# Row norm of an attention layer as a lagged stream of half blocks, and its scores, bias and extreme in one VectorE operation

## The chip, the cores and the metric

The kernel runs on one core of one Trainium2 chip. The metric is device time in microseconds, from start to end of one launch. Before the change it is 35310.41 us (median of three runs, 35305.11 to 35334.66). All data is fp32. The engines are TensorE (matmul, PE in the profile; its weight loads are PEld), VectorE (DVE), ScalarE (ACT), GpSimd (POOL) and SyncE (SP), which issues the DMAs.

## What is computed

Four residual layers over an image of 256 x 256 positions with 128 channels. Each layer normalises its input by groups of 4 channels over all positions, and adds its result to the input. The change is in the first layer, an attention along rows with a norm over channels in front of it:

```
x = x + layer0(group_norm(x))          # then layers 1, 2, 3 in the same way

def layer0(z_ij, ln_gamma, ln_beta, Wq, Wk, Wv, Wb, Wg, Wout):
    mu  = mean(z_ij, channels);  var = variance(z_ij, channels)
    z   = (z_ij - mu) * rsqrt(var + 1e-5) * ln_gamma + ln_beta
    q, k, v = heads(z @ Wq), heads(z @ Wk), heads(z @ Wv)     # 4 heads of 32
    bias = z @ Wb                                             # 4 numbers a position
    g = sigmoid(heads(z @ Wg))
    scores = einsum('bijhd,bikhd->bijkh', q, k) / sqrt(32) + bias[:, None]
    a = softmax(scores, over k)
    o = g * einsum('bijkh,bikhd->bijhd', a, v)
    return o @ Wout
```

The other layers are a selective scan in four directions, a spectral mixing and a recurrence. Most of the time is the scan's; it isn't touched.

## The kernel before

Channels lie on the 128 partitions and positions along the free dimension. An early pass (`stream_stats`, L76) reads all of x and collects statistics; `group_norm_coef` (L52) makes of them one scale and one shift per channel, `ab`. Then `layer0` (L89) has two stages.

**Row norm** (L106 to L142). A loop over 32 blocks of 2048 positions. Per block: load x (L113); VectorE applies the group norm's scale and shift (L114); then for each of four chunks of 512, TensorE multiplies by `cent`, the identity minus 1/128, which takes off the mean over channels (L120, into PSUM); VectorE copies that to `d` in SBUF (L121), ScalarE squares the same PSUM tile (L123), and TensorE averages the squares over channels into one of four groups of 32 partitions of `var` (L124). ScalarE takes the root (L128), VectorE the reciprocal (L129). Then again for each chunk TensorE spreads the reciprocal over the partitions (L135, a matmul with one row of ones), VectorE multiplies (L136), GpSimd applies gamma and beta (L137), TensorE makes the 4 bias rows (L139) and ScalarE copies them (L140). Two DMAs store z and bias to DRAM (L141, L142). Here the scheduler of the language orders the instructions of each engine; the order on each engine is that of the timelines, with two blocks interlaced.

**Attention** (`attention`, L147). It works in 512 units: 32 blocks of 8 image rows, of each row two pairs of heads. The order is written out by hand (`manual_schedule`): at step u every engine's queue gets, one after the other,
- `scores(u + 2)` (L207 to L222): TensorE's four score matmuls into a PSUM tile of 4 x 256 elements, in which the head changes with every matmul; VectorE adds the bias (L215) and takes the negated maximum of each row of 256 (L222);
- `exps(u + 1)`: ScalarE's four exponentials with that maximum as bias, each with its sum over the row (L228); VectorE's reciprocal of the four sums (L231); GpSimd multiplies by it (L232);
- `transposes(u)`: TensorE's eight transposes (L240); ScalarE copies one half (L243), VectorE the other (L245);
- one or, in units 5 to 9 of a block, two `project` calls for the next block (L188, L193; in units 5 to 15);
- `product(u - 1)`: TensorE's four matmuls with v (L254), two heads, each over two halves of k that add up in PSUM; the two heads write different groups of 32 partitions;
- every second unit `gate` (L268), every fourth `out` (L281 to L283), the output matmul, the residual and its statistics.

A matmul of fp32 is two records of the trace. The constants that occur below: `c.ones`, `c.avg128` (all 1/128), `w` (the five weights), `NPOS` = 65536, `CH` = 512.

Of the kernel before, what the change touches and what calls it, by code (L numbers as in the profile page):

```python
# [10 lines left out]
F32 = mybir.dt.float32  # L11
AF = mybir.ActivationFunctionType
ALU = mybir.AluOpType
AX = mybir.AxisListType
PSUM = bass.MemoryType.PSUM
DRAM = bass.MemoryType.DRAM

P = 128
S = 256
NPOS = S * S  # L20
CH = 512
# [24 lines left out]
def load(nc, pool, src, name):  # L46
    to = pool.tile(list(src.shape), F32, name=name)
    nc.sync.dma_start(to, src)
    return to
# [38 lines left out]

def layer0(c, x, x1, ab, stats):  # L89
    tc, nc, t = c.tc, c.nc, c.t  # L90
    BL = 2048
    NB = NPOS // BL
    NH = 4
    with ExitStack() as ctx:
        dram = ctx.enter_context(tc.tile_pool(name="l0_dram", bufs=1, space=DRAM))
        wp = ctx.enter_context(tc.tile_pool(name="l0_w", bufs=1))
        zs = dram.tile([P, NPOS], F32, name="l0_z")
        bs = dram.tile([NH, S, S], F32, name="l0_bias")
        cent = load(nc, wp, t["c_cent"], "l0_cent")
        wb = load(nc, wp, t["l0_wb"], "l0_wb")  # L100
        gamma = load(nc, wp, t["l0_gamma"], "l0_gamma")
        beta = load(nc, wp, t["l0_beta"], "l0_beta")
        w = {n: load(nc, wp, t[f"l0_w{n}"], f"l0_w{n}") for n in "qkvgo"}


        with ExitStack() as a:  # L106
            io = a.enter_context(tc.tile_pool(name="l0a_io", bufs=3))
            wk = a.enter_context(tc.tile_pool(name="l0a_wk", bufs=2))
            ps = a.enter_context(tc.tile_pool(name="l0a_ps", bufs=2, space=PSUM))
            for b in range(NB):  # L110
                sl = bass.ts(b, BL)
                xt = io.tile([P, BL], F32, name="l0a_x")
                nc.sync.dma_start(xt, x[:, sl])  # L113
                nc.vector.tensor_scalar(xt, xt, ab[:, 0:1], ab[:, 1:2], ALU.mult, ALU.add)  # L114
                d = wk.tile([P, BL], F32, name="l0a_d")
                var = ps.tile([P, CH], F32, name="l0a_var")
                for j in range(4):
                    cs = bass.ts(j, CH)
                    dp = ps.tile([P, CH], F32, name="l0a_dp")
                    nc.tensor.matmul(dp, cent, xt[:, cs], start=True, stop=True)  # L120
                    nc.vector.tensor_copy(d[:, cs], dp)  # L121
                    sq = wk.tile([P, CH], F32, name="l0a_sq")
                    nc.scalar.activation(sq, dp, AF.Square)  # L123
                    nc.tensor.matmul(  # L124
                        var[32 * j : 32 * j + 32], c.avg128[:, 0:32], sq, start=True, stop=True
                    )
                rs = wk.tile([P, CH], F32, name="l0a_rs")
                nc.scalar.activation(rs, var, AF.Sqrt, bias=c.eps)  # L128
                nc.vector.reciprocal(rs, rs)  # L129
                bias = wk.tile([NH, BL], F32, name="l0a_bias")  # L130
                for j in range(4):
                    cs = bass.ts(j, CH)
                    r = slice(32 * j, 32 * j + 1)
                    bc = ps.tile([P, CH], F32, name="l0a_bc")
                    nc.tensor.matmul(bc, c.ones[r], rs[r], start=True, stop=True)  # L135
                    nc.vector.tensor_tensor(d[:, cs], d[:, cs], bc, ALU.mult)  # L136
                    nc.gpsimd.tensor_scalar(d[:, cs], d[:, cs], gamma, beta, ALU.mult, ALU.add)  # L137
                    bp = ps.tile([NH, CH], F32, name="l0a_bp")
                    nc.tensor.matmul(bp, wb, d[:, cs], start=True, stop=True)  # L139
                    nc.scalar.copy(bias[:, cs], bp)  # L140
                nc.sync.dma_start(zs[:, sl], d)  # L141
                nc.sync.dma_start(bs.rearrange("h j k -> h (j k)")[:, sl], bias)  # L142

        attention(c, x, x1, zs, bs, w, stats)


def attention(c, x, x1, zs, bs, w, stats):  # L147
# [3 lines left out]
    tc, nc = c.tc, c.nc  # L151
    BL, NH = 2048, 4
    NB = NPOS // BL
    UB = 16
    N = UB * NB
    with ExitStack() as a:
        one = a.enter_context(tc.tile_pool(name="l0b_one", bufs=1))
        io = a.enter_context(tc.tile_pool(name="l0b_io", bufs=2))
        wk = a.enter_context(tc.tile_pool(name="l0b_wk", bufs=2))
        ps2 = a.enter_context(tc.tile_pool(name="l0b_p2", bufs=2, space=PSUM))  # L160
        ps1 = a.enter_context(tc.tile_pool(name="l0b_p1", bufs=1, space=PSUM))
        bias = one.tile([P, NH, 2, S], F32, name="l0b_bias")
# [9 lines left out]
        def load_block(b):  # L172
            k = blocks[b] = {}
            for n, src in (("z", zs), ("x", x)):
                k[n] = io.tile([P, BL], F32, name=f"l0b_{n}")
                nc.sync.dma_start(k[n], src[:, bass.ts(b, BL)])
            for n in "qkg":
                k[n] = wk.tile([P, BL], F32, name=f"l0b_{n}")
            k["v"] = wk.tile([P, 16, P], F32, name="l0b_v")
# [21 lines left out]
        def scores(u):  # L201
            k, r, hp = blocks[u // UB], u % UB // 2, u % 2
            sc = ps2.tile([P, 2, 2, S], F32, name="l0b_sc")
            for jt in range(2):
                for h in range(2):
                    hs = slice(32 * (2 * hp + h), 32 * (2 * hp + h) + 32)
                    nc.tensor.matmul(  # L207
                        sc[:, h, jt],
                        k["q"][hs, bass.ds(r * S + jt * P, P)],
                        k["k"][hs, bass.ts(r, S)],  # L210
                        start=True,
                        stop=True,
                    )
            e = es[u] = wk.tile([P, 4, S], F32, name="l0b_e", bufs=4)
            nc.vector.tensor_tensor(  # L215
                e,
                sc.rearrange("p h j k -> p (h j) k"),
                bias[:, 2 * hp : 2 * hp + 2].rearrange("p h j k -> p (h j) k"),
                ALU.add,
            )  # L220
            top = tops[u] = wk.tile([P, 4], F32, name="l0b_top")
            nc.vector.tensor_reduce(top, e, AX.X, ALU.max, negate=True)  # L222

        def exps(u):
            e, top = es[u], tops.pop(u)
            den = wk.tile([P, 4], F32, name="l0b_den")
            for i in range(4):
                nc.scalar.activation(  # L228
                    e[:, i], e[:, i], AF.Exp, bias=top[:, i : i + 1], accum_out=den[:, i : i + 1]
                )  # L230
            nc.vector.reciprocal(den, den)  # L231
            nc.gpsimd.tensor_tensor(e, e, den[:, :, None].to_broadcast([P, 4, S]), ALU.mult)  # L232
# [14 lines left out]
        def product(u):  # L247
            k, r, hp = blocks[u // UB], u % UB // 2, u % 2
            if hp == 0:
                ops[u // 2] = ps1.tile([P, S], F32, name="l0b_op")  # L250
            for h in range(2):
                hs = slice(32 * (2 * hp + h), 32 * (2 * hp + h) + 32)
                for kt in range(2):
                    nc.tensor.matmul(  # L254
                        ops[u // 2][hs],
                        k["v"][:, 2 * r + kt, hs],
                        ats[u, kt][:, h],
                        start=kt == 0,
                        stop=kt == 1,
                    )  # L260
            for kt in range(2):
                del ats[u, kt]

        def gate(row):
            b, r = divmod(row, 8)
            if r % 2 == 0:
                gates[row // 2] = wk.tile([P, CH], F32, name="l0b_gated")
            nc.vector.scalar_tensor_tensor(  # L268
                gates[row // 2][:, bass.ts(r % 2, S)],
                blocks[b]["g"][:, bass.ts(r, S)],  # L270
                1.0,
                ops.pop(row),
                ALU.add,
                ALU.mult,
            )
# [19 lines left out]
        for u in range(N + 3):  # L295
            b, i = divmod(u, UB)
            if u >= 3 and u % 2 == 1:
                gate((u - 3) // 2)
            if i == 4 and b + 1 < NB:
                load_block(b + 1)  # L300
# [4 lines left out]
            if u < N:  # L305
                transposes(u)
            if 5 <= i and b + 1 < NB:
                project(b + 1, i - 5)
            if 1 <= u <= N:
                product(u - 1)  # L310
            if u >= 5 and (u - 5) % 4 == 0:
                out((u - 5) // 4)
            if 5 <= i < 10 and b + 1 < NB:
                project(b + 1, i + 6)
# [1274 lines left out]
```

## Time and profile before

| | |
|---|---|
| profiled execution | 35314.25 us, its span 35312.4 us |
| median of three runs | 35310.41 us |
| statistics of x | 0 to 87 us; the first 100 us move 366 GB/s |
| group norm's coefficients | 87.5 to 93.6 us |
| row norm | 93.6 to about 751 us |
| attention, projections of the first block | 755 to 806 us |
| attention, the stream of 512 units | 806 to 3499 us |
| layers 1 to 3 | 3499 us to the end |
| VectorE over the whole span | 31875.5 us busy, 90% |
| longest waits in row norm | GpSimd for VectorE's L136 625.2 us, ScalarE's L123 for VectorE's L121 290.4 us, VectorE's L136 for TensorE's L135 149.3 us |
| longest waits in attention | GpSimd's L232 for VectorE's L231 1459.6 us, ScalarE's L243 for TensorE's L240 492.0 us, VectorE's L215 for TensorE's L207 367.5 us, TensorE's L240 for GpSimd's L232 252.0 us |

How to read it: a group's line gives the source line, the engine, the operation, what is written and read, partitions x elements, and how often; in a timeline the first two numbers are start and duration in microseconds, and the brackets at the end give how long the engine was idle before it and which instruction or transfer released it. The ends of matmuls are modelled, so a TensorE that is shown as busy isn't necessarily at its full rate; the starts are measured. PEclk is the share of TensorE's full clock that was granted in a stretch.

### The profile page before, as it was taken

The numbers are of one execution on the slowest core, as the hardware profiler recorded it, in microseconds if no ns is written. First come the engines' busy times: TensorE is split into PE (matmuls) and PEld (weight loads), VectorE is DVE, ScalarE is ACT, GpSimd is POOL, SyncE is SP. The second block draws the span as 40 slices with busy tenths as digits, with TensorE's granted clock in tenths as the row PEclk, the third lists the DMA queues.
The fourth block names the chain that finished last, engine by engine and source line by source line (L and its number), as shares of the span: only waits on it lengthen the run. The fifth ranks groups of instructions, "written<-read, shape, count | busy, mean of one in ns | idle before, by whom it ended". The sixth has DMA issues, their size and how long they took to land. (4 is left out here: it accounts for less than half of the span.)

```text
span 35312.4 us, 252259 instructions
## 1 busy us (share of the span) xinstructions
PE 29559.7 (84%) x72562; PEld 12301.2 (35%) x72562; DVE 31875.5 (90%) x21166; ACT 22600.6 (64%) x46605; POOL 26766.6 (76%) x6540
## 2 busy tenths in 40 slices
PE   7888978888888888888888888888888888878988
PEld 1444433333333333333333333333333333334444
DVE  5777989999999999999999999999999999852599
ACT  2555557777777777777777777777777777532476
POOL 1333069999999999999999999999999999610000
PEclk8999989999999999999999999999999999989888
DMA  3101555555555555555555555555555555675111
GB/s 122 40 37 42 142 173 190 191 191 190 191 190 190 191 190 190 192 191 191 193 201 201 202 201 199 202 201 200 203 201 199 202 202 199 214 204 141 69 33 33
DMA packets 2560588, 5947.56 MB, mean 168 GB/s; under 512 B 898696, under 2 KB 1835417, under 8 KB 1983191
## 3 DMA queue, kind: packets, MB, share of 16 engines
q1 hardware_dynamic: 2424022, 5864.31, 46.1%
q10 hardware_dynamic: 135168, 67.13, 0.6%
q8 instruction: 572, 9.37, 0.1%
q14 instruction: 826, 6.76, 0.1%
HBM read 5238.41 MB, written 692.58 MB: 168 GB/s over the span
## 5 line engine op out<-in xcount | busy, mean ns | idle before, releaser
L675 DVE TENSOR_TENSOR_SCAN l1b_h<-l1b_da,l1b_state,l1b_db 128x1024 f32<-128x1024 f32 x8192 | 18792.7, 2336 | 597.5 <-ACT l1b_db L664 585.4
L690 POOL TENSOR_TENSOR l1b_hc<-l1b_h,l1b_cc 128x2048 f32<-128x2048 f32 x4096 | 18448.6, 4529 | 329.8 <-DVE l1b_h L675 323.4
L709 PE MATMUL l1b_y<-l1b_hc,ident 128*128 128x512 f32 x32768 | 16058.7, 639 | 1117.3 <-POOL l1b_hc L690 1117.3
L660 ACT ACTIVATE l1b_da<-l1b_dl,l_A 128x512 f32<-128x512 f32 (+1 forms) x16384 | 11296.7, 689 | 3153.3 <-DVE l1b_h L675 2845.6
L709 PEld LDWEIGHTS l1b_y<-l1b_hc,ident 128*128 128x128 f32 x32768 | 6527.4, 205 | 10687.0 <-issue 8162.4
L642 POOL TENSOR_TENSOR l1b_db<-l1b_bb,l1b_dus 128x2048 f32<-128x2048 f32 x1536 | 6968.1, 4537 | 1244.3 <-DMA l1b_bb<-l1b_bc 1244.3
L642 DVE TENSOR_TENSOR l1b_db<-l1b_bb,l1b_du 128x2048 f32<-128x2048 f32 x2048 | 4658.9, 2275 | 35.2
L664 ACT ACTIVATE l1b_db<-l1b_state,l1b_db,l1b_af 128x1 f32<-128x1 f32 x8192 | 3045.1, 372 | 0.0
L581 PE MATMUL l1b_mm<-l1b_xd,l_dtw 41*128 41x512 f32 x2048 | 1370.3, 754 | 1700.5 <-ACT l1b_dus L631 1694.7
L607 PE MATMUL l1b_mm<-l1b_tail,ident 128*128 128x512 f32 x2048 | 1297.1, 719 | 1390.1 <-ACT l1b_tail L601 1390.1
L686 ACT COPY l1b_state<-l1b_h 128x4 f32<-128x4 f32 x4095 | 789.5, 193 | 2433.6 <-DVE l1b_h L675 2433.5
L232 POOL TENSOR_TENSOR l0b_e<-l0b_e,l0b_den 128x1024 f32<-128x1024 f32 x512 | 969.1, 1893 | 1774.5 <-DVE l0b_den L231 1459.6
L607 PE MATMUL l1b_mm<-l1b_relu,ident 128*128 128x512 f32 x2048 | 1311.3, 729 | 0.0
L581 PEld LDWEIGHTS l1b_mm<-l1b_xd,l_dtw 41*128 41x128 f32 x2048 | 337.6, 206 | 2515.0 <-ACT l1b_dus L631 2117.7
L631 ACT COPY l1b_dus<-l1b_mm 128x512 f32<-128x512 f32 x512 | 300.1, 586 | 1388.2 <-DVE l1b_db L642 1387.8
L642 DVE TENSOR_TENSOR l1b_db<-l1b_bb,l1b_mm 128x2048 f32<-128x2048 f32 x512 | 1171.5, 2288 | 18.2 <-ACT l1b_dus L631 0.7
L228 ACT ACTIVATE l0b_e<-l0b_e,l0b_top 128x256 f32<-128x256 f32 x2048 | 1014.1, 497 | 210.0 <-DVE l0b_den L231 192.9
L399 DVE SCALAR_TENSOR_TENSOR l1a_mm<-l1a_xi,l1a_each,l1a_mm 128x512 f32<-128x512 f32 x1408 | 1045.9, 755 | 58.3 <-issue 12.5
L607 PEld LDWEIGHTS l1b_mm<-l1b_tail,ident 128*128 128x128 f32 x2048 | 377.7, 207 | 2060.8 <-ACT l1b_tail L601 1816.3
L549 PE MATMUL l1b_du<-l1b_xc,l_xproj 128*40 128x512 f32 x2048 | 981.6, 602 | 62.2 <-DMA l_ds<-in_l_ds 58.2
L215 DVE TENSOR_TENSOR l0b_e<-l0b_sc,l0b_bias 128x1024 f32<-128x1024 f32 x512 | 625.2, 1221 | 370.8 <-PE l0b_sc L207 367.5
L615 ACT COPY l1b_dl<-l1b_mm 128x512 f32<-128x512 f32 x1024 | 588.3, 575 | 524.5 <-DVE l1b_du L623 516.8
(252 smaller groups left out, 29754.5 us busy)
## 6 DMA issues: line engine op xcount, KB each, us to landing
l1b_bb<-l1b_bc SPq DMA_DIRECT2D x2048, 1024.0 KB
l1b_cc<-l1b_bc SPq DMA_DIRECT2D x2048, 1024.0 KB
l1b_xc<-l_xc SPq DMA_DIRECT2D x128, 1024.0 KB
l_y<-l1b_yo SPq DMA_DIRECT2D x128, 1024.0 KB
l1b_xc<-l_xct SPq DMA_DIRECT2D x128, 1024.0 KB
l_y<-l1b_yo SPq DMA_DIRECT2D x256, 512.0 KB
l_xc<-l1a_o SPq DMA_DIRECT2D x64, 1024.0 KB
l_xct<-l1a_ot SPq DMA_DIRECT2D x16, 4096.0 KB
```

The source lines that it names most:

```text
L228: nc.scalar.activation(e[:, i], e[:, i], AF.Exp, bias=top[:, i : i + 1], accum_out=den[:, i : i + 1])
L232: nc.gpsimd.tensor_tensor(e, e, den[:, :, None].to_broadcast([P, 4, S]), ALU.mult)
L399: nc.vector.scalar_tensor_tensor(mm, xis[i][:, r + dy : r + dy + 2, dx : dx + S], each[:, dh, tap : tap + 1], mm, ALU.mult, ALU.add,)
L549: nc.tensor.matmul(du1[:40], w["xproj"][:, dh, k, :], blocks[ch][0][:, dh, cols(ch)], start=dh == 0, stop=dh == 1,)
L581: nc.tensor.matmul(mm, w["dt"][:, chunks[ch][0], dh * P : dh * P + P], xds[ch % 3][0:41], start=True, stop=True,)
L607: nc.tensor.matmul(mm, c.ident, part, start=i == 0, stop=i == 1)
L642: eng.tensor_tensor(db, bbs[g // 2], du[:, None, :].to_broadcast([P, G, CH]), ALU.mult)
L660: nc.scalar.activation(da[:, o + lo : o + hi], dl[:, lo:hi], AF.Exp, scale=w["A"][:, k, dh, n : n + 1])
L664: nc.scalar.activation(first, states[k][:, dh, two : two + 1], AF.Identity, scale=af[:, two : two + 1], bias=first,)
L675: nc.vector.tensor_tensor_scan(h_, a_, d_, states[k][:, dh, one : one + 1], ALU.mult, ALU.add)
L690: nc.gpsimd.tensor_tensor(hc, hs[g], ccs[g // 2], ALU.mult)
L709: nc.tensor.matmul(ys[j % 2], c.ident, hc[:, i], start=False, stop=j // 2 * G + i == 15)
```

## The change

Row norm becomes a function of its own with an order written out by hand. It works on half blocks of 1024 positions. The group norm's scale goes into the centering weights (`scaled`), its shift, centered, into one number per channel (`shift`), which VectorE adds when it copies out of PSUM and ScalarE in the square. Each step of a half block m (or block b) stands in the loop at a fixed lag behind its centering. The four variance matmuls of a block stand together, and so do the four bias matmuls, whose weights are padded to 32 columns so that they write four groups of 32 partitions; four DMAs store the bias.

In attention, the add and the maximum become four `tensor_tensor_reduce` with the operations add and min: each writes -(scores + bias) for 256 elements and the minimum of it. The exponential takes it with scale -1. In the built program each of the four is two VectorE instructions: one that writes 128 x 256, and one that reads out the accumulator, 128 x 1. In `product` the loop over the heads becomes the inner one.

```diff
-        with ExitStack() as a:
-            io = a.enter_context(tc.tile_pool(name="l0a_io", bufs=3))
-            wk = a.enter_context(tc.tile_pool(name="l0a_wk", bufs=2))
-            ps = a.enter_context(tc.tile_pool(name="l0a_ps", bufs=2, space=PSUM))
-            for b in range(NB):
...
+        row_norm(c, x, zs, bs, ab)
         attention(c, x, x1, zs, bs, w, stats)
+
+def row_norm(c, x, zs, bs, ab):
...
+    BL, HL, NH = 2048, 1024, 4
+        io = a.enter_context(tc.tile_pool(name="l0a_io", bufs=4))
+        ps2 = a.enter_context(tc.tile_pool(name="l0a_p2", bufs=2, space=PSUM))
+        ps1 = a.enter_context(tc.tile_pool(name="l0a_p1", bufs=1, space=PSUM))
...
+        nc.tensor.matmul(sp, cent, ab[:, 1:2], start=True, stop=True)
+        nc.vector.tensor_copy(shift, sp)
+        nc.vector.tensor_scalar(scaled, cent, ab[:, 0:1], None, ALU.mult)
...
+        def center(m):
+            b = m // 2
+            dp = dps[m] = ps2.tile([P, 2, CH], F32, name="l0a_dp")
+            for j in range(2):
+                nc.tensor.matmul(
+                    dp[:, j], scaled, half(xs[b], m)[:, bass.ts(j, CH)], start=True, stop=True
+                )
...
+        def keep(m):
...
+            nc.vector.tensor_scalar(
+                half(ds_[b], m), dps[m].rearrange("p j t -> p (j t)"), shift, None, ALU.add
+            )
+        def square(m):
+            sq = sqs[m] = wk.tile([P, 2, CH], F32, name="l0a_sq", bufs=4)
+            nc.scalar.activation(sq, dps.pop(m), AF.Square, bias=shift)
+        def four(name, weights, parts):
+            out = ps1.tile([P, CH], F32, name=name)
+            for j, part in enumerate(parts):
+                nc.tensor.matmul(out[32 * j : 32 * j + 32], weights, part, start=True, stop=True)
+            return out
...
+        def spread(m):
+            bc = bcs[m] = ps1.tile([P, 2, CH], F32, name="l0a_bc")
+            for j in range(2):
+                r = slice(32 * (m % 2 * 2 + j), 32 * (m % 2 * 2 + j) + 1)
+                nc.tensor.matmul(bc[:, j], c.ones[r], rss[m // 2][r], start=True, stop=True)
+        def scale(m):
+            d = half(ds_[m // 2], m)
+            nc.vector.tensor_tensor(d, d, bcs.pop(m).rearrange("p j t -> p (j t)"), ALU.mult)
...
+        for m in range(2 * NB + 10):
+            if m % 2 == 0:
+                late(load_x, m // 2 + 3, NB)
+            late(center, m, 2 * NB)
+            if m % 2:
+                late(var, (m - 3) // 2, NB)
+            late(spread, m - 6, 2 * NB)
+            if m % 2:
+                late(bias, (m - 9) // 2, NB)
+            if m % 2 == 0:
+                late(recip, (m - 4) // 2, NB)
+            late(keep, m - 1, 2 * NB)
+            late(scale, m - 6, 2 * NB)
+            late(square, m - 1, 2 * NB)
+            if m % 2:
+                late(root, (m - 3) // 2, NB)
+                late(bias_out, (m - 9) // 2, NB)
+            late(affine, m - 7, 2 * NB)
...
-            nc.vector.tensor_tensor(
-                e,
-                sc.rearrange("p h j k -> p (h j) k"),
-                bias[:, 2 * hp : 2 * hp + 2].rearrange("p h j k -> p (h j) k"),
-                ALU.add,
-            )
-            nc.vector.tensor_reduce(top, e, AX.X, ALU.max, negate=True)
+            for i in range(4):
+                nc.vector.tensor_tensor_reduce(
+                    e[:, i],
+                    sc[:, i // 2, i % 2],
+                    bias[:, 2 * hp + i // 2, i % 2],
+                    -1.0,
+                    3.0e38,
+                    ALU.add,
+                    ALU.min,
+                    accum_out=top[:, i : i + 1],
+                )
...
                 nc.scalar.activation(
-                    e[:, i], e[:, i], AF.Exp, bias=top[:, i : i + 1], accum_out=den[:, i : i + 1]
+                    e[:, i],
+                    e[:, i],
+                    AF.Exp,
+                    scale=-1.0,
+                    bias=top[:, i : i + 1],
+                    accum_out=den[:, i : i + 1],
                 )
...
-            for h in range(2):
-                hs = slice(32 * (2 * hp + h), 32 * (2 * hp + h) + 32)
-                for kt in range(2):
+            for kt in range(2):
+                for h in range(2):
+                    hs = slice(32 * (2 * hp + h), 32 * (2 * hp + h) + 32)
```

`load_x` loads a block, `var` and `bias` call `four`, `recip` is the reciprocal, `root` the root, `affine` GpSimd's gamma and beta, and `bias_out` copies the bias rows and issues their four DMAs and that of z. `late` calls a step where its index is in range.

## The prediction

> **What bounds the kernel now.** I read first the busy time by stretches, cut where the stages change: row norm from 93.6 us, attention's start at 755, its stream from 806 to 3499. The change touches nothing behind that. Columns: stretch, its length, busy us and instructions of TensorE (PE), its weight loads, VectorE (DVE), ScalarE (ACT) and GpSimd (POOL), then granted clock, DMA share, GB/s.
>
> ```profile
> 93.60:755.00 661.40, 539.31 (x1024) 102.96 (x1024) 313.74 (x321) 167.07 (x288) 124.21 (x128) 0.83 0.27 102
> 806.00:3499.00 2693.00, 2326.34 (x14280) 1294.80 (x14276) 1998.70 (x2808) 1479.22 (x4858) 969.11 (x512) 0.95 0.10 36
> ```
>
> No engine is full in either. Row norm takes 657 us for 32 blocks (93.6 to 751), attention 2693/512 = 5.26 us a unit. So the waits decide, and I read the timelines: first VectorE, then TensorE, over one block of row norm (start us, us, engine, line, operation, count, idle before and its releaser).
>
> ```profile
> 303.37 3.35 DVE L129 RECIPROCAL l0a_rs<-l0a_rs 128x512 f32<-128x512 f32 x1 [2.55 <-ACT l0a_rs L128]
> 306.64 1.22 DVE L121 COPY l0a_d<-l0a_dp 128x512 f32<-128x512 f32 x2
> 308.88 1.28 DVE L136 TENSOR_TENSOR l0a_d<-l0a_d,l0a_bc 128x512 f32<-128x512 f32 x2 [1.02 <-PE l0a_bc L135]
> ...
> 315.00 1.29 DVE L136 TENSOR_TENSOR l0a_d<-l0a_d,l0a_bc 128x512 f32<-128x512 f32 x2 [3.48 <-PE l0a_bc L135]
> ...
> 323.85 3.35 DVE L129 RECIPROCAL l0a_rs<-l0a_rs 128x512 f32<-128x512 f32 x1 [2.55 <-ACT l0a_rs L128]
> ```
>
> ```profile
> 306.77 2.07 PE L135 MATMUL l0a_bc<-l0a_rs,ones 1*128 1x512 f32 x4 [3.11 <-DVE l0a_rs L129]
> 308.78 1.91 PE L124 MATMUL l0a_var<-l0a_sq,avg 128*32 128x512 f32 x2
> 310.49 3.42 PE L139 MATMUL l0a_bp<-l0a_d,l_wb 128*4 128x512 f32 x4
> 313.84 1.13 PE L135 MATMUL l0a_bc<-l0a_rs,ones 1*128 1x512 f32 x4
> 314.89 1.05 PE L124 MATMUL l0a_var<-l0a_sq,avg 128*32 128x512 f32 x2
> ...
> 316.93 1.88 PE L139 MATMUL l0a_bp<-l0a_d,l_wb 128*4 128x512 f32 x4
> ```
>
> To be seen: a block repeats after 323.85 - 303.37 = 20.48 us; TensorE stands 3.11 us for the reciprocal, and is then slow for 7.07 us (306.77 to 313.84): the same four records take 3.42 us, later 1.88. A matmul is two records. Row norm is a chain through all engines, half of it at half clock.
>
> Attention, VectorE and then TensorE over two units:
>
> ```profile
> 2005.21 1.21 DVE L215 TENSOR_TENSOR l0b_e<-l0b_sc,l0b_bias 128x1024 f32<-128x1024 f32 x1
> 2006.45 1.22 DVE L222 TENSOR_REDUCE l0b_top<-l0b_e 128x4 f32<-128x1024 f32 x1
> 2007.59 0.17 DVE L231 RECIPROCAL l0b_den<-l0b_den 128x4 f32<-128x4 f32 x1
> 2007.67 0.66 DVE L245 COPY l0b_at<-l0b_tp 128x512 f32<-128x512 f32 x1
> 2008.25 0.41 DVE L268 SCALAR_TENSOR_TENSOR l0b_gated<-l0b_g,l0b_op 128x256 f32<-128x256 f32 x1
> 2008.58 1.22 DVE L215 TENSOR_TENSOR l0b_e<-l0b_sc,l0b_bias 128x1024 f32<-128x1024 f32 x1
> ```
>
> ```profile
> 2005.86 1.06 PE L254 MATMUL l0b_op<-l0b_at,l0b_v 128*32 128x256 f32 x8
> 2006.85 1.13 PE L207 MATMUL l0b_sc<-l0b_k,l0b_q 32*128 32x256 f32 x8
> 2009.85 1.86 PE L240 MATMUL l0b_tp<-ident,l0b_e 128*128 128x128 f32 x8 [1.86 <-POOL l0b_e L232]
> 2011.64 1.92 PE L254 MATMUL l0b_op<-l0b_at,l0b_v 128*32 128x256 f32 x8
> ```
>
> To be seen: add and maximum hold VectorE for 2007.59 - 2005.21 = 2.38 us, and the reciprocal that GpSimd waits for is queued behind them, though its sums were ready long before. TensorE waits 1.86 us for GpSimd. The chain of two units is: scores(u+2), add and maximum (2.38), reciprocal(u+1), GpSimd(u+1) 1.89, transposes(u+1), product(u), scores(u+4). It holds one add and maximum per two units; the other lies beside GpSimd and TensorE.
>
> **Row norm, part by part.** Removed: the group norm pass L114 (32 x 1.42 = 45 us of VectorE); its scale goes into 128x128 weights, once. Instructions of 512 become 1024; four variance matmuls stand together in four column groups, as do the four for the bias. VectorE per block: 3.35 + two keep and two scale of 1.22 (L215's row for 1024 out of PSUM) = 8.2 us; ScalarE: two squares (0.60 for 512, so about 1.05), root 0.69, copy 0.57 = 3.4; GpSimd 2 x 1.5 (0.77 for 512). None of these would hold 13 us. But VectorE's order is reciprocal, keep, scale in an even half step and keep, scale in an odd one, and the waits make a ring. Zero is the end of an even half step:
> - the keep before it ended at -1.2; the square of the same PSUM tile comes after (as now: ScalarE L123 waits 290 us for VectorE L121) and ends at -0.1. The next centering needs that tile's buffer: it starts at -0.1. Behind this new wait stand variances and spread on TensorE, and VectorE's scale waits for the spread.
> - TensorE, at the slow clock of the rows: two center matmuls 3.4 (to 3.3), four variances 1.7 (to 5.0), two spreads 2.0 (to 7.1). VectorE's keep is over at 1.2; it stands until 7.2 for the spread, scale to 8.4.
> - even half step: reciprocal to 11.8, keep to 13.0, scale to 14.2; square to 14.1. TensorE has done bias, center and spread by about 11.7, and waits some 2.5 us for that square.
> So 14.3 us a block. At full clock the pieces are 1.9, 0.95 and 1.05: scale at 5.1, reciprocal 8.4, period 11.0, again with some 3 us of waiting on TensorE, which is what precedes the slow clock today. [...] I take 13.65, as it lies between the two walks. The variances are not shown four at a time: two at a time would add 1.7 us slow (16.0 a block), four is what I take, since L254's and L135's groups already run side by side as far as the program lets them.
> Of the 74 half steps 16 (filling and draining) lack most work, about 3.3 us each: 58 x 6.83 + 53 + 5 for the first load = 454 us, against 657: **-203**. Ends: 11.0 gives 377 (-280), 16.0 gives 522 (-135).
> DMAs: six per block for three. SyncE issues 4 x 0.27 + 2 x 0.34 = 1.8 us per block, and the loads run three blocks ahead, behind the bias's transfers in the queue; 2 MB per 13.65 us is 154 GB/s, where the statistics' stretch moved 366. I cost it at nothing; if it were not hidden it would be those 1.8 us x 32 = 57. Attention's start is unchanged: it waits for the last bias transfer as now.
>
> **Attention, part by part.** The two instructions become eight in the built program: four of 128x256 and four reads of an accumulator, 128x1. Neither is in this trace. Nearest rows: L268 has the same shape, also with a PSUM input, at 0.41, start to start 0.33; the small reciprocal 0.17, start to start 0.08. So 4 x (0.33 + 0.08) = 1.6 at best, 4 x (0.41 + 0.17) = 2.3 at worst; I take 1.8, a gain of 0.58. The chain has it 256 times; TensorE alone, at full clock, would need about 3.0 us a unit and 1.0 for each projection or output matmul, about 68 of 84 us a block of 16 units, and binds in the units with two projections. I count 0.8: 256 x 0.58 x 0.8 = **-119**. Ends: 0 to -160, and up to 100 more if shorter waits also end the slow stretches (1.92 for 1.06 above).
> [...] Here one source is in PSUM, and L1384 with two f32 SBUF sources (no accumulator) takes 0.69 for 512, full rate. I follow the rows.
> [...] The row says 1.06 for eight at full clock (the second record starts 13 ns after the first): the heads overlap already. Gain 0. Exp with scale -1 is the same instruction (0.49): 0.
>
> Sum: 35314.25 (the profiled execution, span 35312.4) - 203 - 119 = 34992; the median is 3.8 lower: **34990**.
>
> **Rivals.**
> - Both stages stay warm: row norm at 11.0, and the slow stretches of attention vanish: -280 - 119 - 100, about 34810. Against it: the wait ahead of center stays some 3 us. Chance 0.15.
> - The fold is free of gain (2.3 us or more) and the variances go two at a time: -135, about 35175. Chance 0.18.
> - [...] Chance 0.03.
> - [...] Chance 0.03.
> - My forecast, own range 34880 to 35090: chance 0.61.
>
> A measurement here tells about 0.2% (71 us) from no change. Faster 0.94, within 0.03, slower 0.03. The range 34800 to 35170 leaves out part of the warm and of the last cases.
>
> **What would show it.** Row norm: a block period near 13.65, VectorE waiting some 5 us a block for the spread, TensorE 2 to 3 for the square, granted clock still under 0.9; a period of 11 at 0.95 would prove the clock step wrong, 16 the four variances. Attention: fold plus read at 0.45 start to start, groups L254 unchanged at 1.06, pairs of units about 0.5 us shorter. If the product's groups shorten, or the fold takes 0.7, my reading of those rows is wrong.

## The result, and the profile after

The changed kernel takes 34736.12 us (median of four runs, 34735.1 to 34740.03) against 35309.7 us (median of four, 35305.11 to 35334.66) beside it on the same chip: 573.6 us less, a ratio of 0.9836 with a 95% interval of 0.9819 to 0.9853. The prediction was 34990, its range 34800 to 35170. The time lies 64 us below the range.

I split the difference of the two spans (35312.4 - 34733.3 = 579.1 us) by two marks in the traces, the first score matmul and GpSimd's last instruction of attention:

| | before | after | measured gain | predicted |
|---|---|---|---|---|
| to the first score matmul (row norm) | 805.6 | 602.7 | 202.9 | 203 |
| from there to GpSimd's last multiplication (attention's stream) | 2687.8 | 2312.3 | 375.5 | 119 |
| the rest | 31818.9 | 31818.3 | 0.6 | 0 |

The row norm's term came out within a microsecond; attention gained three times what its term said. First the busy time by stretches of the changed kernel, row norm and attention's stream (columns as in the prediction):

```profile
93.60:548.00 454.40, 349.56 (x1026) 93.04 (x1026) 254.43 (x165) 112.05 (x128) 76.74 (x64) 0.74 0.41 149
601.00:2920.00 2319.00, 2194.58 (x14282) 1244.17 (x14282) 1533.15 (x5880) 1438.40 (x4858) 970.00 (x512) 1.00 0.11 42
```

To be seen: row norm's granted clock has fallen from 0.83 to 0.74 although it is faster, and attention's has risen from 0.95 to 1.00. TensorE is now busy for 2194.58 of 2319 us there, 95%, where it was 86%. Row norm's timeline, VectorE and then TensorE over one block:

```profile
254.96 1.22 DVE L187 TENSOR_TENSOR l0a_d<-l0a_d,l0a_bc 128x1024 f32<-128x1024 f32 x1 [5.74 <-PE l0a_bc L183]
256.10 3.35 DVE L177 RECIPROCAL l0a_rs<-l0a_rs 128x512 f32<-128x512 f32 x1
259.36 1.18 DVE L151 TENSOR_SCALAR l0a_d<-l0a_dp,l_shift 128x1024 f32<-128x1024 f32 x1
260.46 1.21 DVE L187 TENSOR_TENSOR l0a_d<-l0a_d,l0a_bc 128x1024 f32<-128x1024 f32 x1
...
268.61 1.22 DVE L187 TENSOR_TENSOR l0a_d<-l0a_d,l0a_bc 128x1024 f32<-128x1024 f32 x1 [5.75 <-PE l0a_bc L183]
```

```profile
257.75 1.13 PE L183 MATMUL l0a_bc<-l0a_rs,ones 1*128 1x512 f32 x4
261.81 3.78 PE L141 MATMUL l0a_dp<-l0a_x,l_scaled 128*128 128x512 f32 x4 [2.93 <-ACT l0a_sq L157]
265.52 1.94 PE L163 MATMUL l0a_var<-l0a_sq,avg 128*32 128x512 f32 x8
...
268.49 1.07 PE L163 MATMUL l0a_bp<-l0a_d,l_wb 128*32 128x512 f32 x8
```

To be seen: the period is 268.61 - 254.96 = 13.65 us. VectorE stands 5.74 us for the spread, TensorE 2.93 us for the square, and right after that wait the centering takes 3.78 us (1.98 elsewhere in the block) and the four variance matmuls 1.94 (the four for the bias, at full clock, 1.07). It is the ring of the prediction, with its two waits; only the pieces differ somewhat (centering 3.78 for 3.4, variances 1.94 for 1.7, spread 1.18 for 2.0, as the clock is full again by then). Attention, VectorE over one unit and TensorE over two:

```profile
2000.85 0.42 DVE L302 CUSTOM_DVE_ANT_0 l0b_e<-l0b_sc,l0b_bias 128x256 f32<-128x256 f32 x1 [0.37 <-PE l0b_sc L291]
2001.20 0.08 DVE L302 DVE_READ_ACCUMULATOR2_ANT l0b_top<- 128x1 f32 x1
2001.20 0.42 DVE L302 CUSTOM_DVE_ANT_0 l0b_e<-l0b_sc,l0b_bias 128x256 f32<-128x256 f32 x1
...
2002.23 0.08 DVE L302 DVE_READ_ACCUMULATOR2_ANT l0b_top<- 128x1 f32 x1
2002.23 0.17 DVE L325 RECIPROCAL l0b_den<-l0b_den 128x4 f32<-128x4 f32 x1
```

```profile
2001.67 1.09 PE L334 MATMUL l0b_tp<-ident,l0b_e 128*128 128x128 f32 x8 [0.87 <-POOL l0b_e L326]
2002.69 1.06 PE L348 MATMUL l0b_op<-l0b_at,l0b_v 128*32 128x256 f32 x8
2003.68 1.13 PE L291 MATMUL l0b_sc<-l0b_k,l0b_q 32*128 32x256 f32 x8
2004.74 1.09 PE L334 MATMUL l0b_tp<-ident,l0b_e 128*128 128x128 f32 x8
2005.77 1.06 PE L348 MATMUL l0b_op<-l0b_at,l0b_v 128*32 128x256 f32 x8
```

To be seen: a fold's accumulator read starts at the same moment as the next fold (2001.20 both), so it adds nothing to the distance of two folds. A fold is 2001.20 - 2000.85 = 0.35 us, four are 2002.23 - 2000.85 = 1.38 us, where 1.8 was taken and the add and the maximum took 2.38. The product's eight records take 1.06, as before. And TensorE's wait for GpSimd is 0.87 us where it was 1.86, with everything behind it at full clock.

This makes a theory in two parts: the fold is shorter than I took it, and TensorE's waits in attention have become too short to bring the slow clock, so the slow stretches are gone. The rivals: the alternating heads bring a part, the new row norm does, or the shorter fold explains all of it by itself.

### The profile page after: what moved, and what is told of

The parts are those of the page before. It is cut to its first block, busy times and chain, and to the rows that moved or that the text cites. A ratio compares the mean times of both kernels' runs of the same rounds, so it can differ in the third digit from the quotient of the medians.

```text
span 34733.3 us, 255526 instructions
## 1 busy us (share of the span) xinstructions
PE 29234.8 (84%) x72564; PEld 12237.5 (35%) x72564; DVE 31351.6 (90%) x24081; ACT 22504.7 (65%) x46445; POOL 26723.0 (77%) x6476
## 3 DMA queue, kind: packets, MB, share of 16 engines
q8 instruction: 572, 9.37, 0.1%
## 5 line engine op out<-in xcount | busy, mean ns | idle before, releaser
L302 DVE CUSTOM_DVE_ANT_0 l0b_e<-l0b_sc,l0b_bias 128x256 f32<-128x256 f32 x2048 | 745.5, 421 | 419.3 <-PE l0b_sc L291 415.9
```

## The experiments

Each run stands beside runs of the kernel before on the same chip. Their medians go from 35305.97 to 35332.29 us, so two runs from different chips can differ by some 25 us for that alone. Where I compare a run with the changed kernel or with another run, I therefore take the stretches of the traces: to the first score matmul, and the stream (from there to GpSimd's last multiplication).

**Each part alone.** The kernel before with only the folds (and the exponential's scale):

```diff
-            nc.vector.tensor_tensor(e, ...bias..., ALU.add)
-            nc.vector.tensor_reduce(top, e, AX.X, ALU.max, negate=True)
+            for i in range(4):
+                nc.vector.tensor_tensor_reduce(e[:, i], ..., ALU.add, ALU.min, accum_out=top[:, i : i + 1])
```

> The kernel before with one part of the change: the four folds a unit in place of add and maximum (and exp with scale -1). Row norm and the product's order are as before. Theory (the fold is 1.38 us a unit where 1.8 was taken, and the shorter waits of TensorE no longer bring slow stretches): all of attention's gain is here, 574 - 206 = 368 us, so about 34940, with attention's granted clock at 0.99 or more. [...] The prediction's own sum was 119 us, about 35190.

Measured: 34940.76 us (34936.79 to 34944.88), ratio 0.9893 (0.9878 to 0.9908). The stream takes 2316.0 us, as in the changed kernel. Its stretch, to be read at the clock:

```profile
806.00:3122.00 2316.00, 2192.70 (x14255) 1252.42 (x14254) 1532.14 (x5876) 1436.52 (x4856) 969.50 (x512) 1.00 0.12 42
```

So the folds alone bring 2687.8 - 2316.0 = 371.8 of attention's 375.5 us, with the old row norm in front. Only the order of the heads:

```diff
-            for h in range(2):
-                hs = ...
-                for kt in range(2):
+            for kt in range(2):
+                for h in range(2):
+                    hs = ...
```

> The kernel before with one part of the change: the product's matmuls alternate between the two heads. Theory (the heads overlapped already, eight records in 1.06 us either way): no change, 35310 within 70 us, and the product's groups at the same length. [...]

Measured: 35290.81 us (35276.06 to 35303.98), ratio 0.9992 (0.9983 to 1.0): nothing that can be told from no change. A product at full clock, where the kernel before had 1.06 too:

```profile
2009.09 1.06 PE L254 MATMUL l0b_op<-l0b_at,l0b_v 128*32 128x256 f32 x8
```

The product's median from first to last start goes from 685 to 678 ns. In this kernel the matmuls of the two heads, which write different groups of 32 partitions, overlap whichever is issued first: eight records take 1.06 us in both orders, and in the kernel before the second starts 13 ns after the first.

Only the new row norm, with the old attention behind it:

```diff
-        with ExitStack() as a:
...
-                nc.sync.dma_start(bs.rearrange("h j k -> h (j k)")[:, sl], bias)
+        row_norm(c, x, zs, bs, ab)
         attention(c, x, x1, zs, bs, w, stats)
```

> The kernel before with one part of the change: the new row norm; attention as before. Theory: a block every 13.65 us and 206 us less, about 35104, attention's clock 0.95 as before. Rival (a part of attention's gain is the row norm's doing, through the bias tile or the clock it starts with): clearly below 35050.

Measured: 35081.76 us (35064.49 to 35085.92), ratio 0.9931 (0.9915 to 0.9948), 239 us less. In its trace the first score comes at 601.6 us, 204 us earlier, and the stream is another 28 us shorter, 2660.0 for 2687.8, with the same instructions in the same order; in the run of the heads alone it is 2667.0. What differs is how many groups of products fall into slow stretches: 15.5% of them before, 11.0% here, 13.1% with the heads. So the old stream's length varies by some 28 us, most likely with where its waits fall, and the run of the folds, with the old row norm in front, shows that attention's 375 us do not need the new one.

**The clock alone.** To take the slow stretches away without touching VectorE, I gave TensorE more to do: in the kernel before, one matmul more of 512 columns in the waits of units 1, 3 and 5 of each block. The transposes write over its result.

```diff
                 tp = ps1.tile([P, 2, 2, P], F32, name=f"l0b_tp{kt}")
+                if kt == 0 and u % UB in (1, 3, 5):
+                    nc.tensor.matmul(tp..., c.ident, bias[:, 0:2, 0], start=True, stop=True)
```

> The kernel before with work added: in units 1, 3 and 5 of each block of 16, one more matmul of 512 columns (some 1.0 us at full clock) on TensorE ahead of the transposes, where it waits 1.95 to 2.23 us for GpSimd; its result is overwritten by the transposes. Nothing on VectorE changes. Theory (waits of this length bring the slow stretches): attention's clock rises from 0.95 to 0.98 or more, and the kernel gets faster by its added work, by about 100 us (0 to 135, the latter being 5% of 2693 us), so about 35210. Rival (all of attention's gain is the shorter fold): no gain, 35310, or up to 96 us slower where the added matmul isn't covered.

Measured: 35216.91 us (35209.57 to 35217.78), ratio 0.9971 (0.996 to 0.9983): 103 us faster by added work; its stream is 2588.2 us for 2687.8, 100 less. Its stream's stretch, and TensorE around two of the added matmuls (L239):

```profile
806.00:3390.00 2584.00, 2320.98 (x14428) 1289.02 (x14426) 1990.92 (x2801) 1478.36 (x4855) 968.00 (x511) 0.99 0.10 38
```

```profile
2029.90 1.12 PE L239 MATMUL l0b_tp<-l0b_bias,ident 128*128 128x512 f32 x2
2031.60 1.09 PE L248 MATMUL l0b_tp<-ident,l0b_e 128*128 128x128 f32 x8 [0.57 <-POOL l0b_e L232]
2032.62 1.06 PE L262 MATMUL l0b_op<-l0b_at,l0b_v 128*32 128x256 f32 x8
...
2038.81 1.12 PE L239 MATMUL l0b_tp<-l0b_bias,ident 128*128 128x512 f32 x2
2040.75 1.09 PE L248 MATMUL l0b_tp<-ident,l0b_e 128*128 128x128 f32 x8 [0.81 <-POOL l0b_e L232]
2041.77 1.06 PE L262 MATMUL l0b_op<-l0b_at,l0b_v 128*32 128x256 f32 x8
```

To be seen: the wait is cut in two by the added matmul, the granted clock is 0.99, and what follows the waits takes 1.09 and 1.06 where the kernel before had 1.86 and 1.92. So the rival that the shorter fold explains all of it by itself falls. The mean distance from GpSimd's start in a unit to its start in the next, worked out from the three traces for each unit of a block (without the first block), shows where (us):

| unit of the block | 0 | 1 | 2 | 3 | 4 | 5 | 6 | 7 | 8 | 9 | 10 | 11 | 12 | 13 | 14 | 15 | sum |
|---|---|---|---|---|---|---|---|---|---|---|---|---|---|---|---|---|---|
| before | 5.05 | 3.38 | 6.85 | 3.38 | 6.06 | 3.38 | 9.37 | 4.94 | 6.04 | 5.01 | 7.90 | 3.86 | 4.86 | 3.92 | 6.18 | 3.69 | 83.87 |
| before, waits filled | 5.05 | 3.38 | 5.78 | 3.38 | 4.47 | 3.38 | 8.22 | 4.94 | 5.98 | 4.98 | 8.32 | 4.21 | 4.65 | 4.10 | 6.18 | 3.69 | 80.71 |
| after | 4.04 | 3.07 | 5.07 | 2.83 | 4.01 | 3.07 | 7.72 | 4.71 | 5.19 | 4.76 | 7.08 | 3.69 | 4.02 | 3.91 | 5.22 | 3.69 | 72.08 |

The filled waits shorten units 2, 4 and 6, by 3.8 us a block; of the others 12 gets 0.21 shorter and 10, 11 and 13 together 0.95 longer, so that 3.2 us a block are left. The folds shorten every even unit, by 0.82 to 1.01 where no slow stretch was involved (0, 8, 10, 12, 14) and by 1.65 to 2.05 in units 2, 4 and 6; the odd units give 1.83 more among them.

**The fold's length by doses.** Was it then wrong to take 0.58 x 0.8 for a fold of 1.8 us? I put VectorE work behind each unit's folds in the changed kernel, a maximum that nobody reads, once as long as the term had it and once (890 numbers for the 333) back to the old 2.38:

```diff
+            idle = wk.tile([P, 1], F32, name="l0b_idle")
+            nc.vector.tensor_reduce(idle, bias...[:, 0:333], AX.X, ALU.max, negate=True)
```

> The changed kernel with VectorE work added behind each unit's four folds: a maximum over 333 numbers into a tile that nobody reads, some 0.42 us start to start by the row of the 1024-wide maximum (1.22 us, its next starts 1.14 later). It brings the fold to the 1.8 us a unit that the prediction took. Prediction's step (a gain of 0.58 a unit is worth 119 us in all): 34736 + 368 - 119 = 34985. Theory: the eight even units of a block get 0.42 longer each and the odd ones a little, 107 to 140 us, and TensorE's waits of 0.98 to 1.21 us grow to 1.4 to 1.6: if that is too short for the slow stretches, 34845 to 34875 with attention's clock at 0.99; if they return already, some 80 more, 34925 to 34955, clock 0.96.

> The same with the maximum over 890 numbers, some 1.00 us: VectorE is held 2.38 us a unit as in the kernel before, by the fold and this. Theory (attention's gain is the time VectorE is held, and what follows from it): attention is as long as before and its clock 0.95 again, 34736 + 368 = 35104, within 40 us. Rival (something else in the new instruction matters, as its releasing the scores' tile or the sums later or earlier, or the clock has another cause): 34950 or less.

Measured: 34862.1 us (34854.87 to 34866.76), ratio 0.9866 (0.9852 to 0.9881), and 35137.09 us (35129.97 to 35144.13), ratio 0.9944 (0.9928 to 0.9961). First the small dose's stream, then the large one's, with TensorE at a wait of the large one:

```profile
601.00:3030.00 2429.00, 2221.35 (x14253) 1253.19 (x14254) 1726.99 (x6387) 1439.45 (x4856) 968.00 (x511) 0.98 0.11 40
```

```profile
604.00:3310.00 2706.00, 2345.62 (x14254) 1302.90 (x14246) 2006.22 (x6388) 1441.76 (x4856) 969.74 (x512) 0.94 0.10 36
```

```profile
2049.52 1.13 PE L291 MATMUL l0b_sc<-l0b_k,l0b_q 32*128 32x256 f32 x8
2052.26 1.09 PE L338 MATMUL l0b_tp<-ident,l0b_e 128*128 128x128 f32 x8 [1.61 <-POOL l0b_e L330]
2053.29 1.82 PE L352 MATMUL l0b_op<-l0b_at,l0b_v 128*32 128x256 f32 x8
2055.03 2.01 PE L379 MATMUL l0b_mm<-l0b_gated,l0b_wo 128*128 128x512 f32 x2
```

To be seen: with VectorE held 2.38 us again the stream is 2706.7 us (2687.8 before), the clock 0.94, and after a wait of 1.61 the product takes 1.82 and the output matmul 2.01. With 1.8 it is 2431.0 and 0.98. So a fold of the length I had assumed would have gained 2687.8 - 2431.0 = 257 us (229, where the old stream is at its shortest, 2660.0), not 119: even on its own premise the term was too small. The count of the waits of TensorE for GpSimd that are over 1.4 us says why:

| | before | large dose | small dose | waits filled | after |
|---|---|---|---|---|---|
| such waits | 97 | 93 | 2 | 3 | 2 |
| three quarters of the waits are below | 1.62 | 1.61 | 1.03 | 0.81 | 0.87 |
| granted clock in the stream | 0.95 | 0.94 | 0.98 | 0.99 | 1.00 |
| products in slow stretches | 15.5% | 13.7% | 3.5% | 0 | 0.4% |

The small dose has 33 waits of 1.27 or 1.28 us and a few slow stretches; with waits of 1.6 and more they are back in full.

Why does a wait of one length bring a slow stretch in one place and none in another? The traces also record when the granted clock changes, and every change lies on a grid of 3.413 us. The kernel before in five steps of that grid, around the waits of 1.62 and 1.86 us (columns as in the prediction: after the length of the step comes TensorE's busy time, and the third number from the end is the granted clock):

```profile
1996.35:1999.76 3.41, 1.79 (x16) 1.34 (x15) 3.38 (x6) 2.08 (x8) 1.89 (x1) 1.00 0.00 0
1999.76:2003.17 3.41, 3.41 (x14) 1.42 (x12) 1.32 (x3) 2.62 (x9) 1.89 (x1) 0.50 0.00 0
2003.17:2006.58 3.41, 3.41 (x26) 1.94 (x24) 2.64 (x4) 0.59 (x1) 0.00 (x0) 1.00 0.37 154
2006.58:2010.00 3.42, 1.56 (x13) 0.84 (x10) 3.39 (x6) 2.08 (x8) 1.89 (x1) 1.00 1.00 331
2010.00:2013.41 3.41, 3.41 (x16) 1.88 (x15) 1.83 (x3) 2.46 (x9) 1.89 (x1) 0.50 1.02 420
```

To be seen: a step in which TensorE is busy for 1.79 or 1.56 of 3.41 us is followed by a step at half clock, one in which it is busy throughout by a step at full clock. So a wait counts by how much of it falls into one step. Over row norm and attention's stream of all twelve traces (without the ends of the stages), 5585 steps at full clock had less than 1.26 us of idle TensorE, and none of them was followed by half clock; 305 had more than 1.76, and all were; of the 337 between, 185 were. The ends of matmuls are modelled, so these bounds are rough.

**A fold with both inputs in SBUF.** The four folds of a unit have one input in PSUM. To see whether that matters I added a fifth fold per unit, with both inputs in SBUF (two parts of the bias), whose results nobody reads:

> [...]

```profile
2003.51 0.42 DVE L302 CUSTOM_DVE_ANT_0 l0b_e<-l0b_sc,l0b_bias 128x256 f32<-128x256 f32 x1
2003.86 0.08 DVE L302 DVE_READ_ACCUMULATOR2_ANT l0b_top<- 128x1 f32 x1
2003.86 0.42 DVE L314 CUSTOM_DVE_ANT_0 l0b_idle<-l0b_bias 128x256 f32<-128x256 f32 x1
2004.20 0.08 DVE L314 DVE_READ_ACCUMULATOR2_ANT l0b_low<- 128x1 f32 x1
```

Measured: 34808.56 us in one run; L314, with both inputs in SBUF, takes 0.42 like L302, and the next instruction starts 0.34 after it. The added 0.345 us a unit lengthened the stream by 80 us, 2392.6 for 2312.3.

**Row norm: is it the clock that holds the period?** In the changed kernel's trace the recorded clock goes two steps of the grid at full and two at half, over and over, and a block takes 13.65 us, four steps, from the second block on, the last one apart. These steps of 3.413 us are the windows of the two expectations below. One block:

```profile
253.88:260.70 6.82, 5.00 (x20) 1.33 (x20) 5.74 (x4) 1.32 (x3) 1.20 (x1) 1.00 0.32 120
260.70:267.53 6.83, 5.72 (x14) 1.52 (x14) 2.17 (x2) 2.18 (x3) 1.20 (x1) 0.50 0.55 192
```

Two edits of the changed kernel. In the first the reciprocal moves to the odd half step, in the second TensorE gets two more matmuls of 512 columns per block in its wait, into a PSUM tile that the bias overwrites:

```diff
-            if m % 2 == 0:
-                late(recip, (m - 4) // 2, NB)
             late(keep, m - 1, 2 * NB)
+            if m % 2:
+                late(recip, (m - 5) // 2, NB)
```

> The changed kernel with row norm's reciprocal moved from the head of the even half step to the odd one, behind its keep, where VectorE waits 5.7 us for the spread. Theory (the even half step's ring of reciprocal, keep, square, centering sets the period, and the wait it makes for TensorE brings the slow clock): the 2.9 us wait goes, TensorE stays at full clock, and VectorE's 8.2 us and TensorE's 7.8 us a block are what is left: a block in 8.5 to 10.3 us, the latter if it locks to three windows of 3.413 us; 97 to 150 us less than 34736, so about 34610 with row norm's clock at 0.95. Rival (TensorE stays slow all the same, with its 14.2 us of work a block at the slow clock): no change, 34736, or some 16 us slower.

```diff
             late(spread, m - 6, 2 * NB)
+            if m % 2 == 0 and 6 <= m < 2 * NB:
+                fill = ps1.tile([P, CH], F32, name="l0a_bp")
+                for j in range(2):
+                    nc.tensor.matmul(fill, c.ident, xs[m // 2][:, 0:CH], start=True, stop=True)
```

> The changed kernel with work added: in each even half step of row norm, behind the spread, two more matmuls of 512 columns on TensorE (1.9 us at full clock) into the bias's PSUM tile, which nobody reads before the bias overwrites it. They lie in the 2.93 us that TensorE waits for the square. Theory (that wait brings the slow clock, and the slow clock the period of 13.65): TensorE stays at full clock and the block takes the 11.0 us of the walk at full clock, 29 x 2.65 = 77 us less, about 34660. Rival (the period is set by the ring whatever the clock, or by the length of the gate's windows): 13.65 stays and the time is 34736, or up to 14.3 and some 20 us slower.

Measured: 34594.68 us (34584.34 to 34599.74), ratio 0.979 (0.9776 to 0.9805), with the reciprocal moved; 34668.1 us (34660.69 to 34675.54), ratio 0.9812 (0.9797 to 0.9826), with the added matmuls. TensorE with the added matmuls (L221), over one block:

```profile
254.35 1.98 PE L221 MATMUL l0a_bp<-l0a_x,ident 128*128 128x512 f32 x4
257.35 1.98 PE L141 MATMUL l0a_dp<-l0a_x,l_scaled 128*128 128x512 f32 x4 [1.01 <-ACT l0a_sq L157]
259.26 1.06 PE L163 MATMUL l0a_var<-l0a_sq,avg 128*32 128x512 f32 x8
...
265.28 1.98 PE L221 MATMUL l0a_bp<-l0a_x,ident 128*128 128x512 f32 x4
```

To be seen: a block takes 265.28 - 254.35 = 10.93 us; the walk at full clock had said 11.0. Same ring, same VectorE, more work for TensorE, and the first score comes 78 us earlier (524.5 for 602.7; 77 expected). Between 119 and 443 us its trace has no step at half clock. With the reciprocal moved, VectorE over two blocks:

```profile
250.99 3.35 DVE L177 RECIPROCAL l0a_rs<-l0a_rs 128x512 f32<-128x512 f32 x1
...
260.27 3.34 DVE L177 RECIPROCAL l0a_rs<-l0a_rs 128x512 f32<-128x512 f32 x1
...
268.25 3.34 DVE L177 RECIPROCAL l0a_rs<-l0a_rs 128x512 f32<-128x512 f32 x1
```

Two blocks take 268.25 - 250.99 = 17.26 us, 8.63 each, against the 8.2 that VectorE needs; TensorE's longest wait is 1.27 us, once in two blocks, and from 130 to 368 us its trace has one step at half clock. The first score comes at 452.1 us, 151 us earlier than in the changed kernel (97 to 150 expected). This version beats both kernels. The two edits show what held the period; they do not part the row norm's 203 us among the pass taken out, the larger instructions and the new order.

**The reciprocal ahead of the fold.** The prediction said that the fold is on the chain because the small reciprocal is queued behind it. On the version above, with the two calls changed over:

```diff
-            if u + 2 < N:
-                scores(u + 2)
             if u + 1 < N:
                 exps(u + 1)
+            if u + 2 < N:
+                scores(u + 2)
```

> The kernel with the reciprocal of row norm in the odd half step (34595), and in attention one step moved: the exponentials of unit u+1, with the small reciprocal and GpSimd's instruction, stand ahead of the scores and folds of unit u+2 in the program, so that VectorE's reciprocal is no longer queued behind a fold. Nothing is added. Theory (the fold sits on the chain only by standing in front of that reciprocal): GpSimd starts up to 1.38 us earlier where VectorE is not itself waiting for the sums, TensorE's waits for GpSimd (71 us under its own name and 178 under its weight loads, in the changed kernel's stream) mostly go, and the time falls by 50 to 110 us, the latter nearly all of the 125 us that TensorE stands idle: about 34515. Rival (VectorE, now waiting for the sums with the fold behind it, hands the scores on later, and the exponentials of the next unit with them): no gain, 34595, or slower.

```profile
446.00:2709.00 2263.00, 2180.65 (x14263) 1241.23 (x14262) 1526.38 (x5876) 1444.00 (x4857) 969.15 (x512) 1.00 0.12 43
```

Measured: 34530.59 us (34523.49 to 34538.47), ratio 0.9781 (0.9765 to 0.9797), the fastest of all. The version above ran on another chip; by the traces the stream went from 2310.8 to 2261.3 us, 49.5 us less, at the lower end of what was expected. The medians differ by 64 us; by the traces 16 us more lie in layers 1 to 3 and 5 ahead of the stream, where the edit changes nothing. TensorE is busy for 2180.65 of 2263 us, 96%. Its waits for GpSimd in the stream (us in total, how many, the longest), first in the version above and then here:

```profile
PE l0b_tp L334 <- POOL l0b_e L326: 72.2, 100, 2.5
PE l0b_tp L334 <- POOL l0b_e L326: 4.2, 2, 2.5
```

So the fold did sit on the chain by standing in front of the reciprocal, as the prediction said.

## Why the prediction was right and wrong

- **Row norm, -203: right, and for its reasons, with some luck in the last digits.** The stage gained 202.9 us, with the period that was taken and the two waits and the slow clock that the walk gave. The agreement to a microsecond is luck: 14.3 instead of 13.65 would have made it 58 x 0.32 = 19 us less, and the 53 us for filling and draining were an estimate with no row behind it. The 13.65 of the sum was the author's estimate, and no run of the kernel before shows it; the changed kernel's trace showed it, 13.65 us, four steps of the recorded clock's grid. Periods are not always whole numbers of steps, though: with the waits filled it is 10.93 (3.2 steps), with the reciprocal moved 8.63 (2.5). In these runs the period locked only where a slow stretch lies in every block (20.48 us before, six steps, and 13.65 after). Two readings of the kernel before were rough: its slow stretch is 6.83 us by the recorded clock, two steps, not 7.07, and it is a third of the block, not half.
- **Four variances at once, DMAs at nothing:** right; 1.94 us for the four at the slow clock, and only the first load is waited for in the changed kernel's row norm (TensorE, 2.5 us, where 5 was counted).
- **Heads alternate, 0:** right (0.9992, 0.9983 to 1.0), by the row: eight records in 1.06 us in both orders.
- **The fold, 1.8 us and 0.8 of it on the chain, -119: the step that failed.** The mechanism was right, the size was not, in three ways. (1) 1.8 for four folds was too long: "1.6 at best" added 0.08 for each accumulator read, but the read runs beside the next fold, so the best was 1.38 and the gain per unit 1.00, not 0.58. 256 x 1.00 x 0.8 = 205. (2) "Up to 100 more if shorter waits also end the slow stretches" was written down as an end and put at nothing in the sum, without a reason. It happened, and filling the waits alone measures it at about 100 us (2687.8 - 2588.2 in the stream). (3) The remaining 375 - 205 - 100 = 70 us are the factor: 0.8 should have been about 1.07. By the table, even units without a slow stretch gain 0.9 us of the 1.00 on average, and the odd ones, counted at nothing, 1.83 us a block, 59 us in all. The fifth fold gives 80/(256 x 0.345) = 0.91 and the small dose 119/(256 x 0.42) = 1.1 for the factor. How much belongs to (2) and how much to (3) is known only roughly: taken from the table, (3) leaves 375 - 256 x 0.9 - 59 = 86 us for (2), and the added matmuls may themselves cost something. The sign that the prediction named, pairs of units about 0.5 us shorter, came out at 1.47 ((83.87 - 72.08)/8).
- **What should have been seen in the profile before.** The prediction itself quoted a wait of 1.86 us followed by records of 1.86 and 1.92 for 1.09 and 1.06. Taking 0.58 us from each such wait leaves 1.3, which by the small dose is enough: 2 waits over 1.4 us were left of 97. The sum treated the wait and the slow stretch behind it as two things, and paid for one.
- **The rival "both stages stay warm", 34810,** lies nearest to the result, by two errors that cancel: it named the end of the slow stretches in attention but had 219 us there for 375.5, and 280 us in row norm, which did not stay warm, for 202.9. The other three had no part in it.

## What to carry to other kernels

Where a profile shows a stretch of TensorE at half clock right behind a wait, price the wait together with the stretch: shortening the wait until the stretch is gone pays twice (here the wait went from 1.86 to 0.87 us, and the product behind it from 1.92 to 1.06). To test it before any rework, put idle matmuls into the wait and see whether the kernel gets faster. And a result that the next engine waits for should not be queued behind work that nobody waits for yet; moving one call was worth about 50 us here.

## What the runs showed of the hardware

- In attention, waits of TensorE for GpSimd of up to 1.06 us (39 of 1.00 to 1.06 in the kernel before) left it at full clock; with 33 waits of 1.27 or 1.28 us (the small dose) 3.5% of the products fell into slow stretches; of the kernel before's 62 waits of 1.62 or 1.63 us 43 were followed by half clock within 3.4 us, and of its 32 of 1.86 or 1.87 all. In row norm, 1.01 left it at full clock (the added matmuls), 1.27 with one exception (the reciprocal moved), and 2.93 did not (the changed kernel). The recorded clock changes on a grid of 3.413 us, and by the count above what decides is the idle time within one step, with the bound between 1.26 and 1.76 us.
- A VectorE accumulator read (0.08 us) starts together with the next fold and adds nothing to the distance of two folds, 0.345 us for 128 x 256, with one input in PSUM or both in SBUF alike.
